# Three PSUM banks of two kinds of piece used as one ring

## The chip, the cores and the metric

The kernel runs on one core of one Trainium2 chip. The metric is the device time of one execution in microseconds (us); where several executions were timed, their median is given. The core's engines are PE (matrix products, with PEld loading the stationary operand), DVE (elementwise work and reductions), ACT (activations and copies), POOL (elementwise work on SBUF and indirect DMA) and SP (which issues most DMAs). PE writes its products to PSUM[...]; DVE and ACT empty them.

## What is computed

Two layers of a transformer-like block in float32, on 2048 tokens of 512 channels. The reference, cut to its skeleton:

```python
xn = layernorm(x)
x = x + lightning_attention(xn, qkv_w, out_w, gate_w, norm_w) + moe(xn, router, experts, shared)
xn = layernorm(x)
x = x + attention(xn, Wqkv, bqkv, Wo, bo) + routed_low_rank(xn, A, B, Wr)
```

In layer 0, the attention has 32 heads of 128 with exponential decay and no softmax:

```python
qkv = silu(h @ qkv_w.T)
scores = einsum('bhnd,bhmd->bhnm', q, k) * decay
attn = einsum('bhnm,bhmd->bhnd', scores, v)      # in blocks, with a carried state
out = (sigmoid(h @ gate_w.T) * norm_w * rms_normalized(attn)) @ out_w.T
```

The mixture has 16 experts of inner width 128, of which each token takes two, and a shared one: `h = silu(x @ w1 + b1) * (x @ w2 + b2)`, then `gate * (h @ w3 + b3)`. Layer 1 has softmax attention with one head of 128 and 64 low-rank adapters of rank 16, of which each token takes sixteen.

## The kernel before

The tokens are cut into four chunks of 512 (`NCH`). The kernel runs in three stages.

The opening normalizes and transposes the chunks, computes the shared expert and the router's choice, and works out at which row of a buffer each token goes for its experts.

Layer 0 then goes over the chunks i, and in each over eight groups g of four heads (a "unit"), and in each over seven parts p (`ORDER`), because the big projections to q, k, gate and v are made with Strassen's seven products of half-size blocks instead of eight (the `Outer` class; `product`, line 667, is its matrix product; sums of blocks are made on DVE and POOL). Chunk 0 uses the plain products and makes the weight sums that later chunks reload. Between the parts, the kernel places smaller pieces of work from a list: `later(after, f)` puts a piece down for so many slots later, and `slot()`, called after every block product, takes one piece that is due. So the order on PE is written out by hand. The pieces are:

- `Quarter.scores` (lines 770 and 771): q times k for two heads, read by DVE, which multiplies by the decay (line 97 is the helper `tt` through which all elementwise operations of two tensors go, on DVE or POOL)
- `Quarter.attend` (lines 782 and 783): scores times v, read by ACT (squares for the norm, lines 794 and 797) and by DVE (gate, line 802)
- `Unit.project` (line 859) and, in chunk 0 and the last unit, `project_plain` (line 879): the output projection, added to the accumulator `acc` by DVE, or copied by ACT in the first group (lines 867 and 888)
- `Expert.turn`, `up` and `down` (lines 707, 717 and 729) for one tile of 128 expert rows: a transpose (read by DVE, line 709), the two up products (read by ACT for `h`, line 724, and then by DVE for `he`, line 725), and the down product, copied by ACT (line 734).

Layer 1 goes over the chunks again. For each it runs low-rank products by the same seven-product scheme (`seven`, lines 1423 and 1493), and between them the pieces of attention: the transposes (line 243), the router (1305), q and k (1299), v (1345), scores and softmax (1357), the gates' transpose (1379), the probabilities' transpose (1442), and the output product `attended` (1468). The router, q, k, scores and so on of the next chunk are called its "head".

A piece gets its PSUM bank from a pool by a tag. A tag has a number of buffers, and a piece that asks for one waits until the piece that had it is released, that is, until its last reader is done. The eight banks before: two for tag `a`, one each for `b` and `e` (the big products), two for `sc`, one for `o` (scores times v) and one for `y`. Tag `sc` serves scores, the experts' transposes and up products, half of the output projections and all the head pieces of layer 1; tag `y` serves the experts' down products, the other half of the output projections, and line 1468. In `project`, for example:

```python
py = ps_sc() if p in ("p7", "p5", "p2") else ps_y()
```

A scheduler orders the instructions from the program's order, and may move one ahead of another that still has to wait for a buffer. In layer 0 the engines' orders follow the list of pieces.

Of the kernel before, what the change touches and what calls it, by code (L numbers as in the profile page):

```python
# [9 lines left out]
FP = mybir.dt.float32  # L10
# [8 lines left out]
P = 128  # L19
# [47 lines left out]
def block_kernel(  # L67
# [38 lines left out]
    ps = ctx.enter_context(tc.tile_pool(name="ps", bufs=1, space=PSUM))  # L106
# [21 lines left out]
        return stage.tile([P, C + WROW], FP, tag="xw", name=name)  # L128

    def ps_sc():  # L130
        return ps.tile([P, 512], FP, tag="sc", name="ps_sc", bufs=2)

    def ps_o():
        return ps.tile([P, 512], FP, tag="o", name="ps_o", bufs=1)

    def ps_y():
        return ps.tile([P, 512], FP, tag="y", name="ps_y", bufs=1)


    opening = ExitStack()  # L140
# [124 lines left out]
    def route(xT, ge, sel):  # L265

        full = [P, TPC, E]
        pl = ps_sc()
        for t in range(TPC):
            for c in range(NC):  # L270
# [58 lines left out]
    def shared_down(i, hT):  # L329
        xc = xs[i]  # L330
        pg = ps_sc()
        for t in range(TPC):
            nc.tensor.transpose(pg[0 : E + 1, bass.ts(t, P)], gates[i][:, t, :], ident)
        gT = work.tile([E + 1, CH], FP, tag="geT", name="geT", bufs=1)
        nc.scalar.copy(gT, pg[0 : E + 1, :])
        for t in range(TPC):
            py = ps_mm()
            mm(py, gT[:, bass.ts(t, P)], b3_t, start=True, stop=False)
            for e in range(SH):
                mm(py, hT[:, e, bass.ts(t, P)], w3sh[:, e, :], start=False, stop=(e == SH - 1))  # L340
            tt(xc[:, t, :], py, xc[:, t, :], ALU.add)
# [135 lines left out]
    for i in range(NTT):  # L477
        tt(cum[:, i + 1, :], cum[:, i, :], sel_all[:, i, :], ALU.add)
    pp = ps_sc()
    flat = "p t e -> p (t e)"  # L480
    at = NTT * E
# [118 lines left out]
    with tc.tile_pool(name="attn", bufs=1) as attn:  # L600
# [89 lines left out]
        class Expert:  # L690
# [36 lines left out]
            def down(self):  # L727
                py = ps_y()
                mm(  # L729
                    py, self.he, self.we[:, 2 * NC * INTER : 2 * NC * INTER + C],  # L730
                    start=True, stop=True,
                )
                ye = attn.tile([P, C], FP, tag="sum", name="ye", bufs=3)
                nc.scalar.copy(ye, py)
                nc.sync.dma_start(out=yd[bass.ts(self.j, P), :], in_=ye)
# [75 lines left out]
        class Unit:  # L811
# [43 lines left out]
            def project(self, p):  # L855
                py = ps_sc() if p in ("p7", "p5", "p2") else ps_y()
                for t in range(2):
                    for hh in range(2):
                        mm(  # L859
                            py[:, bass.ts(t, S)], self.O[p][:, hh, bass.ts(t, P)], self.wo[p][:, hh, :],  # L860
                            start=(t == 0 and hh == 0), stop=(hh == 1), skip_group_check=True,
                        )
                if self.i not in acc:
                    acc[self.i] = accp.tile([P, 7, 2, C // 2], FP, tag="acc", name="acc")
                o = acc[self.i][:, SEVEN.index(p)].rearrange("p t c -> p (t c)")
                if self.g == 0:
                    nc.scalar.copy(o, py)
                else:
                    add(o, py, o)
                if p == "p3":  # L870
                    if (self.i, self.g) == (NCH - 1, NG - 2):
                        combine(self.i)
                    self.done()

            def project_plain(self, b, pair, gT, t):
                py = ps_sc() if t else ps_y()
                for h in range(2):
                    for hh in range(2):
                        mm(  # L879
                            py[:, bass.ts(h, S)], gT[:, hh, bass.ts(t, P)], self.wo[pair, h][:, hh, :],  # L880
                            start=(h == 0 and hh == 0), stop=(hh == 1), skip_group_check=True,
                        )
                if self.i not in acc:
                    acc[self.i] = accp.tile([P, 7, 2, C // 2], FP, tag="acc", name="acc")
                o = acc[self.i][:, 2 * b : 2 * b + 2, t]
                py = py.rearrange("p (h c) -> p h c", h=2)
                if self.g == 0 and pair == 0:
                    nc.scalar.copy(o, py)
                else:
                    add(o, py, o)  # L890
                if (pair, b, t) == (1, 0, 1):
                    self.done()
# [710 lines left out]
```

## Time and profile before

| | us |
|---|---|
| median of 3 runs | 2904.78 (2901.41 to 2913.6) |
| the profiled execution | 2910.55 |
| its span in the profile | 2908.9 |

By stage, from the busy times by stretch of the profiled execution:

| stretch, us | what | PE busy | DVE busy | ACT busy | POOL busy | PE clock granted |
|---|---|---|---|---|---|---|
| 0 to 177 | opening | 151.0 | 109.8 | 54.0 | 85.1 | 0.92 |
| 177 to 809 | layer 0, chunk 0 | 618.4 | 377.0 | 145.3 | 363.2 | 0.99 |
| 809 to 1400 | layer 0, chunk 1 | 576.1 | 285.2 | 227.5 | 323.2 | 1.00 |
| 1400 to 2000 | layer 0, chunk 2 | 594.6 | 298.1 | 238.3 | 303.5 | 1.00 |
| 2000 to 2601 | layer 0, chunk 3 | 580.0 | 305.9 | 230.5 | 328.6 | 0.99 |
| 2601 to 2909 | layer 1 | 291.0 | 177.3 | 57.5 | 65.9 | 0.99 |

The chunks' borders are rounded. A wait row of the profile reads "engine, tile and line that waited <- engine, tile and line that ended it: us in total, times, longest". A row of the timeline has start, length, engine, line, operation, the tiles as out<-in, and in brackets how long the engine was idle before it and what ended that. A float32 product appears as two matrix instructions.

### The profile page before, as it was taken

To read this page: it belongs to the slowest core of one execution; us is meant where nothing else is said; L and a number is where in the kernel's file an instruction comes from. 1 tells how busy PE (TensorE), PEld (TensorE's weight loads), DVE (VectorE), ACT (ScalarE), POOL (GpSimd) and SP (SyncE) were. 2 spreads that over 40 slices of the span, in tenths; PEclk is the share of its full clock that TensorE was granted. 3 is DMA by queue.
4 is the path that set the end of the run, shared out by engine and by line. 5 is a ranking of instruction groups with operands and counts; after the bars stand their busy time and mean duration, and the time that the engine had idled before them with its cause. 6 is when DMAs were issued, how large, how long until landed. Compare 5 with 4: busy or idle time off the path is not lost.

```text
span 2908.9 us, 49460 instructions
## 1 busy us (share of the span) xinstructions
PE 2811.0 (97%) x19864; PEld 2570.9 (88%) x19864; DVE 1553.3 (53%) x2615; ACT 953.1 (33%) x1683; POOL 1469.4 (51%) x1213
## 2 busy tenths in 40 slices
PE   8989999999999999999999999999999989999999
PEld 4469999999989999999999999999999979987877
DVE  7555666666544545444545555555445455558463
ACT  3312222221244333333443333333433334332111
POOL 4535666565445555555645555445444665554110
PEclk9999999999999999999999999999999999999999
DMA  7788998888987777777777777777777776653111
GB/s 263 291 307 329 350 350 344 342 333 329 368 319 258 277 251 262 260 264 277 285 263 258 257 259 260 261 280 282 282 257 257 282 297 225 224 213 96 60 60 60
DMA packets 161942, 763.20 MB, mean 262 GB/s; under 512 B 18209, under 2 KB 24225, under 8 KB 109874
## 3 DMA queue, kind: packets, MB, share of 16 engines
q1 hardware_dynamic: 149826, 706.25, 65.7%
q0 software_dynamic: 11888, 53.79, 5.3%
q8 instruction: 157, 2.57, 0.4%
q14 instruction: 71, 0.58, 0.1%
HBM read 596.14 MB, written 163.05 MB: 261 GB/s over the span
## 4 chain that ended last, share of the span: by engine, by line
PE 78%; DVE 9%; DMA 4%; issue 4%; POOL 2%; ACT 1%; SPq 0%; DVEq 0%; POOLq 0%; ACTq 0%
PE ps_a L667 22%; PE ps_e L667 11%; PE ps_b L667 7%; PE ps_y L859 5%; PE ps_sc L859 4%; PE ps_o L782 3%; PE ps_sc L770 3%; PE ps_sc L717 2%; PE ps_y L879 2%; PE ps_sc L879 2%; DVE c L97 2%; PE ps_a L1493 2%; PE ps_o L783 2%; PE ps_sc L771 2%; PE ps_y L729 1%
## 5 line engine op out<-in xcount | busy, mean ns | idle before, releaser
L667 PE MATMUL ps_a<-xt,w 128*128 128x128 f32 x5376 | 752.9, 276 | 15.0 <-DVE r L97 7.4
L667 PEld LDWEIGHTS ps_a<-xt,w 128*128 128x128 f32 x5376 | 683.1, 193 | 36.4 <-issue 14.9
L97 POOL TENSOR_TENSOR c<-c,r 128x512 f32<-128x512 f32 x240 | 323.7, 1366 | 186.3 <-DVE r L97 138.7
L745 ACT ACTIVATE c<-c 128x512 f32<-128x512 f32 x256 | 161.3, 630 | 656.7 <-DVE c L97 360.2
L667 PE MATMUL ps_e<-xt,w 128*128 128x128 f32 x2688 | 374.3, 275 | 2.0 <-DVE c L97 1.3
L97 POOL TENSOR_TENSOR c<-c 128x512 f32<-128x512 f32 x216 | 270.7, 1269 | 184.6 <-DVE c L97 182.6
L97 POOL TENSOR_TENSOR w<-w 128x512 f32<-128x512 f32 x224 | 292.9, 1322 | 133.4 <-DVE w L97 67.8
L667 PEld LDWEIGHTS ps_e<-xt,w 128*128 128x128 f32 x2688 | 344.7, 192 | 12.4 <-issue 4.1
L97 POOL TENSOR_TENSOR sums<-sums,sq 128x512 f32<-128x512 f32 x120 | 154.3, 1286 | 386.5 <-ACT sq L797 386.1
L667 PE MATMUL ps_a<-w,xt 128*128 128x128 f32 x1792 | 346.9, 275 | 0.0
L997 ACT COPY cp<-ps_a 128x512 f32<-128x512 f32 x336 | 195.0, 580 | 426.9 <-PE ps_a L667 426.9
L667 PEld LDWEIGHTS ps_a<-w,xt 128*128 128x128 f32 x1792 | 272.6, 192 | 0.0
L97 DVE TENSOR_TENSOR c<-ps_a,c 128x512 f32<-128x512 f32 x232 | 158.0, 687 | 214.5 <-PE ps_a L667 213.5
L667 PE MATMUL ps_b<-xt,w 128*128 128x128 f32 x1680 | 236.3, 277 | 4.8 <-ACT c L1011 4.2
L802 DVE SCALAR_TENSOR_TENSOR gT<-ps_o,nw,c 128x256 f32<-128x256 f32 x256 | 111.9, 479 | 226.5 <-ACT sq L797 222.4
L667 PEld LDWEIGHTS ps_b<-xt,w 128*128 128x128 f32 x1680 | 216.9, 194 | 16.1 <-issue 5.5
L859 PE MATMUL ps_y<-wo,gT 128*128 128x256 f32 x736 | 175.4, 381 | 0.6 <-DVE acc L97 0.6
L667 PE MATMUL ps_e<-w,xt 128*128 128x128 f32 x896 | 173.5, 275 | 0.0
L770 PE MATMUL ps_sc<-c 128*128 128x256 f32 x512 | 154.1, 383 | 11.3 <-DVE he L725 7.7
L97 DVE TENSOR_TENSOR s<-ps_sc,decay 128x384 f32<-128x384 f32 x256 | 139.1, 551 | 39.0 <-PE ps_sc L771 37.7
L782 PE MATMUL ps_o<-s,c 128*128 128x256 f32 x512 | 153.8, 382 | 4.3 <-DVE s L97 4.2
L859 PEld LDWEIGHTS ps_y<-wo,gT 128*128 128x128 f32 x736 | 132.8, 190 | 15.5 <-issue 0.7
(307 smaller groups left out, 4768.1 us busy)
## 6 DMA issues: line engine op xcount, KB each, us to landing
w<-in_w_att_dram SPq DMA_DIRECT2D x128, 1024.0 KB
st<-in_w_att_dram SPq DMA_DIRECT2D x32, 1024.0 KB
wo<-in_w_out_dram SPq DMA_DIRECT2D x113, 256.0 KB
decay<-dec SPq DMA_DIRECT2D x64, 384.0 KB
w<-ws0p SPq DMA_DIRECT2D x12, 1792.0 KB
w<-ws1p SPq DMA_DIRECT2D x12, 1792.0 KB
w<-ws2p SPq DMA_DIRECT2D x12, 1792.0 KB
w<-ws3p SPq DMA_DIRECT2D x12, 1792.0 KB
```

Source lines behind the costliest of these rows:

```text
L97: (eng or nc.vector).tensor_tensor(o, a, b, op)
L667: mm(bank[:, bass.ts(ty, P)], a, b, start=(first and ty == 0), stop=True, skip_group_check=True,)
L717: mm(pu[:, bass.ts(n, P)], w12[:, n, c, :], self.xeT[:, c, :], start=(c == 0), stop=(c == NC - 1),)
L745: nc.scalar.activation(qk, qk, AF.Silu)
L770: mm(p[:, 0:S], self.c[:, 2 * hh, P : 2 * P], q, start=True, stop=True)
L771: mm(p[:, S : S + P], self.c[:, 2 * hh + 1, P : 2 * P], q[:, 1, :], start=True, stop=True,)
L782: mm(po[:, bass.ts(hh, S)], v[:, 0, :], self.s[:, hh, 0:S], start=True, stop=False)
L783: mm(po[:, hh * S + P : (hh + 1) * S], v[:, 1, :], self.s[:, hh, S:], start=False, stop=True,)
L802: nc.vector.scalar_tensor_tensor(gT[:, h, :].rearrange("p (t n) -> p t n", t=2), po[:, bass.ts(h, S)].rearrange("p (t n) -> p t n", t=2), ...
L859: mm(py[:, bass.ts(t, S)], self.O[p][:, hh, bass.ts(t, P)], self.wo[p][:, hh, :], start=(t == 0 and hh == 0), stop=(hh == 1), skip_group_c ...
L879: mm(py[:, bass.ts(h, S)], gT[:, hh, bass.ts(t, P)], self.wo[pair, h][:, hh, :], start=(h == 0 and hh == 0), stop=(hh == 1), skip_group_ch ...
L997: nc.scalar.copy(c, bank)
```

## The change

The tag `sc` gets a third buffer, and `ps_y()` hands out a buffer of `sc` instead of one of its own tag, which is gone. The total stays at eight banks. All pieces that took `sc` or `y` now share three banks and take them in turn.

```diff
     def ps_sc():
-        return ps.tile([P, 512], FP, tag="sc", name="ps_sc", bufs=2)
+        return ps.tile([P, 512], FP, tag="sc", name="ps_sc", bufs=3)

     def ps_o():
         return ps.tile([P, 512], FP, tag="o", name="ps_o", bufs=1)

     def ps_y():
-        return ps.tile([P, 512], FP, tag="y", name="ps_y", bufs=1)
+        return ps_sc()
```

Pieces that were named `ps_y` in the profile are named `ps_sc` after the change.

## The prediction

> **What bounds the kernel now.** I read the page first, then the waits of PE, then the stretches around those waits in order of time. The page's first part:
>
> ```profile
> PE 2811.0 (97%) x19864; PEld 2570.9 (88%) x19864; DVE 1553.3 (53%) x2615; ACT 953.1 (33%) x1683; POOL 1469.4 (51%) x1213
> ```
>
> PE has work in 97% of the span, and no other engine is above 53%. So 2908.9 - 2811.0 = 97.9 us of PE's idle time is about all that a new bank order can give back. The waits of PE (us in total, times, longest) say who ended it:
>
> ```profile
> PE ps_sc L859 <- DVE gT L802: 7.8, 1, 7.8
> PE ps_sc L770 <- DVE he L725: 7.7, 7, 3.2
> ...
> PE ps_y L729 <- DVE acc L97: 5.8, 6, 1.0
> ...
> PE ps_y L1468 <- DVE spare L97: 4.0, 2, 2.3
> PE ps_y L729 <- ACT acc L867: 3.8, 3, 1.5
> ...
> PE ps_sc L770 <- DVE acc L97: 3.2, 1, 3.2
> ```
>
> The reader is to see two kinds of wait. L859 waits for gT, which it multiplies: data. L770 does not read he, and L729 and L1468 do not read acc or spare: each waits until the reader named has emptied the bank that it is to write. With the small rows of the same kind (0.6 and 0.3 in layer 0, 0.6 and 0.4 in layer 1) these bank waits make 21.4 us in layer 0 (19 stalls) and 5.0 us in layer 1. From 879 to 1347 us they come as a pair in every unit of 77.8 us. One pair:
>
> ```profile
> 926.59 0.35 DVE L725 SCALAR_TENSOR_TENSOR he<-ps_sc,xw,h 128x128 f32<-128x128 f32 x1 [0.95 <-ACT h L724]
> 927.09 0.67 PE L770 MATMUL ps_sc<-c 128*128 128x256 f32 x2 [0.74 <-DVE he L725]
> ...
> 956.70 0.35 DVE L725 SCALAR_TENSOR_TENSOR he<-ps_sc,xw,h 128x128 f32<-128x128 f32 x1 [4.54 <-ACT h L724]
> 956.97 0.68 DVE L97 TENSOR_TENSOR acc<-ps_y,acc 128x512 f32<-128x512 f32 x1
> 957.70 0.30 PEld L729 LDWEIGHTS ps_y<-xw,he 128*128 128x128 f32 x2 [1.16 <-DVE acc L97]
> 957.70 1.12 PE L729 MATMUL ps_y<-xw,he 128*128 128x512 f32 x2 [0.97 <-DVE acc L97]
> ```
>
> At 927.09 scores wait for the expert's up product, two ps_sc pieces back, which DVE could not read before ACT had made h. At 957.70 the down product waits for the one ps_y bank; but it reads he too, and he was ready only at 957.05, 0.65 us before. The longest bank wait, and what it costs besides:
>
> ```profile
> 578.01 4.71 DVE L97 TENSOR_TENSOR w<-w 128x512 f32<-128x512 f32 x3
> 582.65 0.68 DVE L97 TENSOR_TENSOR acc<-ps_sc,acc 128x512 f32<-128x512 f32 x1
> 583.25 0.67 DVE L97 TENSOR_TENSOR c<-ps_e,c 128x512 f32<-128x512 f32 x1
> 583.38 1.18 PE L770 MATMUL ps_sc<-c 128*128 128x256 f32 x2 [3.24 <-DVE acc L97]
> ```
> ```profile
> 583.30:587.00 3.70, 3.62 (x15) 3.44 (x16) 3.50 (x7) 0.00 (x0) 3.00 (x3) 0.54 0.42 49
> 587.00:600.00 13.00, 13.00 (x102) 12.54 (x101) 8.08 (x12) 0.60 (x1) 8.33 (x7) 1.00 0.98 394
> ```
>
> The last two are the busy times by stretch (PE, PEld, DVE, ACT, POOL, then the granted clock): after the stall PE ran at 0.54, so it lost another 3.70 x 0.46 = 1.7 us.
>
> [...] the trace agrees after the stalls of 3.24 us at 583 and 3.25 at 848 (0.63 from 848.5 to 853.1, 1.7 us lost), and shows half clock after the 2.28 us one at 2647 too[...].
>
> **The change, part by part.** No computing instruction or DMA is added or removed, and no queue but PE's gets new conditions in layer 0: there the order on all five engines is the old one. What changes is which piece each of the 711 pieces of the two kinds waits for. Before: the ps_sc piece two back, or the ps_y piece one back. After: in 696 cases the piece three back, whichever kind (in layer 1 a dozen take the bank that came free first).
>
> What is taken away, layer 0. A stall's gap understates it: running products overlap (six start in 0.83 - 0.28 = 0.55 us, so 0.11 apart, each lasting 0.275), so each costs its gap plus 0.16. The 19 stalls cost 21.4 + 19 x 0.16 = 24.5 us. Does the new condition stall instead? I set the first product of each piece against the end of the last reader of the piece three back, both from the trace of before. The middle distance is 8 us, the smallest in layer 0 is 0.98 us, and for the stalled pieces it is 4.3 us or more. So no new bank wait in the places as they are. What stays is data: the seven L729 stalls between 879 and 1347 keep their wait for he, 1.13 lost and only 0.60 gained each, so 7 x 0.53 = 3.7 us stay. That leaves 20.8 us, and with the two half-clock windows (2 x 1.7) 24.2 us.
>
> What is late next. PE gains only until it meets another bank whose reader does not follow PE.
> - At 583: DVE is held by its weight sums until 582.65 whatever PE does. PE would be 5.1 us early (3.4 + 1.7) at its next ps_e group (587.57 before, so 582.5), and that bank is read by DVE until 583.92. It waits about 1.5 us there. Net 3.6.
> - At 848: the ps_a group of 852.40 needs the bank that ACT copies until 849.06, in a chain that started before the stall: 3.3 of 5.1 us stay.
> - The six L770 stalls of 0.9: the next tight bank (933.8) has 0.75 us to spare, so up to 0.16 is lost each, 0.9 in all.
> - L729 at 1455 and 2046 (1.6 each): ACT is behind there, and the ps_a group at 1460.65 has 0.65 us to spare: 1.9 of 3.2 is lost.
> Sum given back: 1.5 + 1.8 + 0.9 + 1.9 = 6.1. Layer 0 gains 24.2 - 6.1 = 18.1 us. Later the other engines follow, since they are idle about half the time and wait for PE's products.
>
> Layer 1 (from 2601). Here the order moves, because a piece may be placed while a third bank is free. Five low-rank products (0.43 us each) that stood before and between the first head's products now follow them; PE has 2.48 us to wait there for k, which ACT makes after its softmax work for the router, and two of the five filled PE's time before that wait: 0.9 us lost. The three L1468 stalls of the first chunk (2.8 us of gaps and a half-clock window) go, but DVE has no idle time there between 2643 and 2652, and the next ps_e group needs its copy of 2651.04: I count 0.5. At 2797 the stall goes (1.68) and with it 1.14 us for which DVE itself waited for that product. The group behind it, though, waits for DVE already:
>
> ```profile
> 2803.27 0.68 DVE L97 TENSOR_TENSOR cp<-ps_e,cp 128x512 f32<-128x512 f32 x1
> ...
> 2804.01 1.13 PE L1423 MATMUL ps_e<-t,fa 128*128 128x256 f32 x4 [1.66 <-DVE cp L97]
> ```
>
> so I count 1.1 there, and 0.6 for the L243 wait at 2812. Sum -0.9 + 0.5 + 1.1 + 0.6 = 1.3, with 5 either way, since the order of DVE and ACT moves too. The two built programs also differ in PE's waits on its own earlier products (380 for 326); all stand four or more products back, and the waits of PE charge those of before with 0.8 us in all, so I take nothing, with 2 us as the upper bound.
>
> Total 18.1 + 1.3 = 19.4 us. The profiled execution took 2910.55 us (span 2908.9), 5.8 above the median of the runs, 2904.78. Taken from the median: 2904.8 - 19.4 = 2885.4, say 2886.
>
> **Rivals.** A: everything is given back elsewhere. For: DVE and ACT chains do end several of the stalls, and the give-back above was followed only to the next tight bank. Against: DVE 53% and ACT 33% busy, and no tight bank between the pairs. If two thirds of layer 0's 24.2 us are given back and layer 1 gives nothing, 8 us stay: 2897. B: little is given back, and layer 1's waits go as well: 24.2 + 5.0 + 1.7 = 31 us, 2874. Against it: the DVE work at 578 and 2643 does not depend on PE. C, slower: layer 1's order. Its three head chains have less low-rank work between them, and DVE, which bounds the chunk boundaries (32.6 us busy of 36 between 2780 and 2816), now makes gathered-row sums ahead of the copy that PE waits for. Price: the five products of 0.43, three boundaries of about 1.5, and two half-clock windows of 1.7, together 10 us; it decides only if layer 0 keeps under 10 of its 18. With 4 kept: 2911. That the change does not do what it says can be left aside: the ring of three is in the built program.
>
> **How the numbers follow.** Forecast 0.52, A 0.30, B 0.12, C 0.06. A measurement of this kernel tells 0.5%, 14.5 us, from no change. The forecast's own spread (14 to 25 us) is nearly all on the faster side, A mostly within the bound, B faster, C half within it and half beyond: faster 0.60, same 0.36, slower 0.04. The range goes from B's end, 2872, to just short of no gain, 2903: the runs of before differ by 12 us among themselves.
>
> **What would show it.** PE's idle time falls from 97.9 to about 80 us; rows of L770, L729 and L1468 waiting for he, acc or spare vanish, but for about 0.4 us each of L729 waiting for he. The clock stays at 1.00 around 583 and 848. Stalls of 1 to 2 us appear at a ps_e group near 583 and a ps_a group near 848, ended by DVE and ACT. Units of 77.8 us become about 76.4. I am wrong if those units keep their length, or if layer 1, 308 us now, grows by more than 5.

## The result and the profile after

| | before | changed |
|---|---|---|
| median, 10 runs each, us | 2909.24 (2896.75 to 2920.75) | 2890.01 (2882.67 to 2903.62) |
| the profiled execution, us | 2910.55 | 2889.33 |
| its span, us | 2908.9 | 2887.6 |

The ratio is 0.9944, with a 95% interval of 0.992 to 0.9967. Measured again beside later runs, the changed kernel gave 0.9953 (0.994 to 0.9966). In the profile after, PE does the same work in less time; the page's first part:

```profile
PE 2808.7 (97%) x19864; PEld 2571.3 (89%) x19864; DVE 1555.9 (54%) x2615; ACT 952.4 (33%) x1683; POOL 1467.2 (51%) x1213
```

PE's idle time is 2887.6 - 2808.7 = 78.9 us, 19.0 less than before. The waits of PE (us in total, times, longest):

```profile
PE ps_e L1423 <- DVE cp L97: 8.8, 2, 6.5
PE ps_sc L859 <- DVE gT L802: 5.2, 1, 5.2
...
PE ps_sc L729 <- DVE he L725: 4.1, 8, 1.6
...
PE ps_e L667 <- DVE c L97: 3.3, 4, 1.2
```

There is no row of L770 or L1468 any more, and L729 waits only for he, which it multiplies. (In a second profiled execution of the changed kernel one wait of L1468 for spare, of 1.1 us, is left.) One unit of chunk 1 in the timeline, the one that was shown of before around 927:

```profile
875.09 1.13 PE L729 MATMUL ps_sc<-xw,he 128*128 128x512 f32 x2 [0.31 <-DVE he L725]
...
921.38 0.60 PE L770 MATMUL ps_sc<-c 128*128 128x256 f32 x2
921.41 0.35 ACT L724 ACTIVATE h<-ps_sc,xw 128x128 f32<-128x128 f32 x1
921.79 0.35 DVE L725 SCALAR_TENSOR_TENSOR he<-ps_sc,xw,h 128x128 f32<-128x128 f32 x1 [0.95 <-ACT h L724]
...
951.30 1.12 PE L729 MATMUL ps_sc<-xw,he 128*128 128x512 f32 x2 [0.36 <-DVE he L725]
```

DVE still waits 0.95 us for ACT's h before it can make he, as before. But scores (L770) now start before he is made, because they write to another bank. The unit takes 76.2 us (875.1 to 951.3 at L729) instead of 77.8. At the two long stalls of before:

```profile
581.59 0.60 PE L770 MATMUL ps_sc<-c 128*128 128x256 f32 x2
...
587.82 0.94 PE L667 MATMUL ps_e<-xt,w 128*128 128x128 f32 x6 [1.19 <-DVE c L97]
...
847.56 1.12 PE L729 MATMUL ps_sc<-xw,he 128*128 128x512 f32 x2 [1.60 <-DVE he L725]
```
```profile
581.00:586.00 5.00, 5.00 (x43) 4.90 (x42) 5.00 (x5) 0.00 (x0) 4.45 (x3) 1.00 0.92 358
847.00:852.00 5.00, 4.44 (x32) 3.91 (x33) 3.26 (x6) 4.01 (x8) 4.40 (x5) 1.00 0.92 333
```

The granted clock (third number from the end of the lower lines) is 1.00 in both places, where it had been 0.54 and 0.63 after the stall; and in each a shorter stall has come in its place, of 1.19 and 1.60 us.

Where the time went is read best by taking the same instruction of PE in both traces (layer 0's order is the same) and subtracting its starts. The table gives how much each kernel gained on before's profiled execution in each stretch, in us; the last two columns are the first two experiments below.

| stretch of before, us | changed | ring in layer 0 only | ring in layer 1 only |
|---|---|---|---|
| 0 to 177, opening | -4.3 | -5.4 | -1.2 |
| 177 to 570 | 0.2 | 0.0 | 0.7 |
| 570 to 720 (stall at 583) | 2.7 | 3.1 | 0.6 |
| 720 to 809 | 2.3 | 3.4 | 3.6 |
| 809 to 870 (stall at 848) | 3.3 | 3.3 | -1.3 |
| 870 to 1350 (a pair of stalls a unit) | 10.1 | 10.1 | -0.1 |
| 1350 to 2370 | 3.9 | 2.9 | 0.0 |
| 2370 to 2578 | 5.3 | 5.2 | 1.4 |
| 2578 to the end, layer 1 | -2.3 | 2.6 | -0.1 |
| sum | 21.2 | 25.2 | 3.6 |

### The profile page after: what moved, and what is told of

The parts are those of the page before. It is cut to its first block, busy times and chain, and to the rows that moved or that the text cites. A ratio compares the mean times of both kernels' runs of the same rounds, so it can differ in the third digit from the quotient of the medians.

```text
span 2887.6 us, 49441 instructions
## 1 busy us (share of the span) xinstructions
PE 2808.7 (97%) x19864; PEld 2571.3 (89%) x19864; DVE 1555.9 (54%) x2615; ACT 952.4 (33%) x1683; POOL 1467.2 (51%) x1213
## 4 chain that ended last, share of the span: by engine, by line
PE 84%; DVE 7%; DMA 4%; issue 2%; POOL 2%; ACT 1%; SPq 0%; DVEq 0%; POOLq 0%; ACTq 0%
PE ps_a L667 24%; PE ps_e L667 12%; PE ps_sc L859 9%; PE ps_b L667 7%; PE ps_sc L879 4%; PE ps_o L782 4%; PE ps_sc L770 3%; PE ps_sc L717 3%; PE ps_a L1493 2%; PE ps_o L783 2%; PE ps_sc L771 2%; PE ps_sc L729 1%; DVE c L97 1%; PE ps_a L1423 1%; DVE r L97 1%
## 5 line engine op out<-in xcount | busy, mean ns | idle before, releaser
L667 PE MATMUL ps_a<-xt,w 128*128 128x128 f32 x5376 | 751.0, 276 | 18.0 <-DVE r L97 9.3
L667 PEld LDWEIGHTS ps_a<-xt,w 128*128 128x128 f32 x5376 | 681.5, 192 | 38.3 <-issue 14.0
L667 PE MATMUL ps_e<-xt,w 128*128 128x128 f32 x2688 | 374.0, 275 | 3.5 <-DVE c L97 3.3
L97 POOL TENSOR_TENSOR w<-w 128x512 f32<-128x512 f32 x224 | 293.5, 1325 | 137.9 <-DVE w L97 74.3
L667 PEld LDWEIGHTS ps_e<-xt,w 128*128 128x128 f32 x2688 | 344.2, 192 | 14.1 <-DVE c L97 4.2
L667 PE MATMUL ps_a<-w,xt 128*128 128x128 f32 x1792 | 346.5, 275 | 0.0
L859 PE MATMUL ps_sc<-wo,gT 128*128 128x256 f32 x1288 | 306.6, 381 | 5.2 <-DVE gT L802 5.2
L667 PEld LDWEIGHTS ps_a<-w,xt 128*128 128x128 f32 x1792 | 272.2, 192 | 0.0
L97 DVE TENSOR_TENSOR acc<-ps_sc,acc 128x512 f32<-128x512 f32 x208 | 143.1, 689 | 232.7 <-PE ps_sc L859 163.5
L859 PEld LDWEIGHTS ps_sc<-wo,gT 128*128 128x128 f32 x1288 | 233.5, 191 | 30.7 <-DVE gT L802 5.4
L667 PE MATMUL ps_b<-xt,w 128*128 128x128 f32 x1680 | 235.8, 277 | 4.7 <-ACT c L1011 4.2
L667 PEld LDWEIGHTS ps_b<-xt,w 128*128 128x128 f32 x1680 | 216.5, 193 | 15.8 <-issue 5.5
L667 PE MATMUL ps_e<-w,xt 128*128 128x128 f32 x896 | 173.2, 275 | 0.0
```

Source lines behind the costliest of these rows:

```text
L97: (eng or nc.vector).tensor_tensor(o, a, b, op)
L667: mm(bank[:, bass.ts(ty, P)], a, b, start=(first and ty == 0), stop=True, skip_group_check=True,)
L859: mm(py[:, bass.ts(t, S)], self.O[p][:, hh, bass.ts(t, P)], self.wo[p][:, hh, :], start=(t == 0 and hh == 0), stop=(hh == 1), skip_group_c ...
```

## The experiments

Theory T: the gain is the removal of bank waits in layer 0, at their own price. The rivals are named with the runs. Kernels that carry the helper of the first experiment have their lines moved by 15 or 16, so that L785 is L770, L744 is L729, L874 is L859, L682 is L667, L1439 is L1423 and L1484 is L1468.

**The ring in one layer alone.** Both kernels have before's tags and take them in turn where `ring_on` says so; it is switched just before layer 1's first head. (`bank_sc()` hands out before's two buffers of `sc`, `bank_y()` its one of `y`.)

```diff
+    def in_turn(own):
+        if not ring_on[0]:
+            return own()
+        turn_of_ring[0] += 1
+        return (bank_y, bank_sc, bank_sc)[turn_of_ring[0] % 3]()
...
     def ps_sc():
-        return ps.tile([P, 512], FP, tag="sc", name="ps_sc", bufs=2)
+        return in_turn(bank_sc)
...
     def ps_y():
-        return ps.tile([P, 512], FP, tag="y", name="ps_y", bufs=1)
+        return in_turn(bank_y)
...
+    ring_on[0] = False
     head = Head(0)
```

> The ring of three is used in layer 0 only; layer 1 has the old banks (two for the one kind, one for the other). Theory T (the gain is the bank waits of layer 0): the whole gain of the change stays, 18 to 24 us, a ratio of 0.992 to 0.994 to the kernel before, and PE's waits at lines 770 and 729 for he or acc are gone, while the waits of line 1468 for spare (4 to 5 us) stay. Since layer 1 lost 1.7 us with the ring, this version should be as fast as the changed kernel or up to 2 us faster. Rival R (the gain comes from layer 1's other order): 1.000.

Measured: 2883.07 us median, a ratio of 0.9919 (0.9895 to 0.9942). As expected, PE has no wait of L770 for he or acc and none of L729 for acc left, and L1468 still waits for spare (4.2 us). The other way round, with `ring_on` false first and true in layer 1:

> The ring of three is used in layer 1 only; layer 0 has the old banks. Theory T: a ratio of 0.999 to 1.001, layer 1 between 0 and 3 us longer: its line 1468 no longer waits for spare, but DVE is behind there and line 1423 waits for cp instead (about 9 us in two waits). The 21 us of bank waits in layer 0 stay. Rival R (the gain comes from layer 1's other order): 0.994.

Measured: 2908.02 us median, 1.0013 (1.0002 to 1.0024), that is 0.6 to 7 us slower than before. The waits of PE with the ring in layer 1 only:

```profile
PE ps_sc L785 <- DVE he L740: 7.7, 7, 3.2
PE ps_e L1439 <- DVE cp L97: 6.7, 2, 4.4
PE ps_sc L874 <- DVE gT L817: 6.6, 1, 6.6
PE ps_y L744 <- DVE acc L97: 5.8, 6, 1.0
```

Layer 0's bank waits are what they were before, and layer 1's longer wait for cp is there (2.8 us in two before). So the whole gain lies in layer 0, rival R falls, and the ring in layer 1 costs a little. The third column of the table is of use for a second reason: this kernel has before's banks in layer 0, so what it gained there, 4.9 us between 177 and 2578, is not the ring. Most of it (3.6) stands at 726, where before's profiled execution waited 2.04 us for gT and then ran at a clock of 0.66 for 5 us, and this one did not wait; in the nine other profiled executions that wait is anything from 0 to 1.65 us. Against this kernel the changed one gained 27.8 - 4.9 = 22.9 us in layer 0. Five profiled executions in all have the ring of three in layer 0 with PE's order unchanged. From 177 to 2578 they gained 25.5 to 28.8 us on before's execution, so 20.6 to 23.9 on this one.

**The up products in the single bank.** Before's tags, and in `Expert.up`:

```diff
-                pu = ps_sc()
+                pu = ps_y()
```

> The banks of before, two for the one kind and one for the other, but the experts' up products take the single bank (y) in place of one of the pair (sc). The order of the instructions is that of before. Theory T (it is a matter of which reader stands before a piece in its bank, three pieces back being enough): the waits of line 770 for he go (from 12 to about 4 us in all), but line 859's output products and line 729 then stand behind an up product in the one bank, and by the times of the trace line 859 gets some 40 us of waits of a kind that it had not; slower than before by 10 to 30 us, 1.004 to 1.010. Rival S (taking the up products off the pair of banks is what gains): 0.996 or lower.

Measured: 2938.04 us median, 1.012 (1.0093 to 1.0146). The waits of PE:

```profile
PE ps_y L859 <- DVE he L725: 35.6, 17, 3.0
...
PE ps_sc L770 <- DVE acc L97: 1.9, 2, 1.2
```

L770 no longer waits for he, but the output products do, 17 times. Between 870 and 2578 this kernel fell from 10.5 us ahead of before to 25.2 behind, 35.7 us, close to what that row says. What was expected came out, a little past its dear end (33 us slower for 10 to 30); rival S falls.

**A ring of two.** The changed kernel with `bufs=2` for `bufs=3`, one of the eight banks being left unused.

> All pieces of both kinds in one ring as in the changed kernel, but of two banks[...]. Theory T (the third bank back is what counts): by the times of the changed kernel's trace every piece two back leaves 23 us of bank waits in layer 0, as much as before (22), so a ratio of 0.998 to 1.002. Rival U (sharing itself, that a piece is not tied to a kind, is the gain): 0.994 to 0.996. Rival V (a bank less costs more than the order of turns gains): above 1.005.

Measured: 2895.14 us median, 0.996 (0.9949 to 0.9971): about half of the changed kernel's gain, at the edge of what rival U gave and outside T's. The waits of PE say why:

```profile
PE ps_sc L770 <- DVE he L725: 7.7, 7, 3.2
...
PE ps_sc L859 <- DVE s L97: 5.4, 1, 5.4
...
PE ps_sc L729 <- DVE he L725: 2.6, 7, 0.4
```

The waits of L770 for he are all there: scores stand two pieces behind the up product, and two banks are too few. The waits of L729 for acc are gone: they came from the tie of the down product to the one bank y, and the turn of two removes them; in the trace that is 0.6 us in each of seven units. So U is right for one of the two waits of the pair; the other stays when two banks are taken in turn. The step of T that failed is the count of 23 us of waits. The trace has 16.3 us of bank waits in layer 0, and the longest, 5.4 at L859, only replaces waits that stood behind it before: those for s (2.36), c (1.32) and cp (0.86) are gone and the one for gT is 2.0 shorter. PE was 5.3 us behind before's execution ahead of this place and 4.7 behind after it. Why the other 7 us of the count did not appear is open. (This profiled execution took 2912.78 us, 17 above its median, because it lost 16 us before 177: the clock in 120 to 180, third from the end, was 0.72. From 177 to 2578 it gained 12.2 us on before's.)

```profile
120.00:180.00 60.00, 56.85 (x109) 21.24 (x110) 18.41 (x38) 7.57 (x10) 17.27 (x31) 0.72 0.61 232
```

**Two and one, but sorted otherwise.** Before's tags; the up products take y, and all output projections take sc. Layer 1 is as before.

```diff
-                pu = ps_sc()
+                pu = ps_y()
...
-                py = ps_sc() if p in ("p7", "p5", "p2") else ps_y()
+                py = ps_sc()
...
-                py = ps_sc() if t else ps_y()
+                py = ps_sc()
```

> No ring: two banks of the one kind and one of the other, as before, but with other pieces in them. The experts' up and down products have the single bank to themselves in layer 0, and all output projections, scores and transposes share the pair. Theory T (only the distance in time between a bank's reader and its next writer counts): the changed kernel's trace, taken over to these banks, leaves 10.9 us of bank waits in layer 0 of the 21.6, of which 6 are at output products (lines 859 and 879) that wait for data next anyway, as in the ring of two; so the waits at 729 for acc go, those at 770 fall to about 4 us, and the time is 12 to 20 us under before, 0.993 to 0.996. Rival W (the ring's freedom to take any bank is needed): 0.999 or more.

Measured: 2885.69 us median, 0.9941 (0.9919 to 0.9963), the changed kernel's own ratio, without a ring. The waits of PE:

```profile
PE ps_sc L859 <- DVE s L97: 4.3, 1, 4.3
...
PE ps_y L729 <- DVE he L725: 4.1, 8, 1.6
PE ps_sc L770 <- DVE acc L97: 3.9, 3, 2.5
```

Rival W falls: what counts is how long ago a bank's last reader was due when the next piece comes, and a sorting that puts the slowly read pieces (up, down) behind one another does that nearly as well. In layer 0 (177 to 2578) it gained 21.3 us on before's execution, the ring of three 25.5 to 28.8; layer 1, where it has before's banks, gained 5.1 us in this execution and lost 2.3 in the changed kernel's, which would make up for that. The pairs and the stall at 848 gave as much as with the ring (13.3 us from 809 to 1350 for 13.2 to 13.4); from 2370 to 2578, where L859 now waits for s, it gained 1.6 us and the ring 3.9 to 5.7.

**The data wait that stays.** The ring in layer 0 only, and the down product one slot later.

```diff
-            later(14, e.down)
+            later(15, e.down)
```

> The ring of three in layer 0 only, and the experts' down product due one slot later (15 for 14). Theory T: what stays of the stalls at line 729 is its wait for he (4.1 us in 8 stalls in the changed kernel), a wait for data that a later place removes; so this row goes and the time is 3 to 5 us under that of the ring in layer 0 with 14: a ratio of 0.9900 to 0.9915. If the bank behind it (the one that down leaves later) now comes late, the row goes and the time stays at 0.992.

Measured: 2885.76 us median, 0.9928 (0.99 to 0.9957): not better than with 14 by the median, though the interval does not exclude what was expected. The row L729 waiting for he is gone, and these have grown in its place (1.6 and 1.1 us with 14):

```profile
PE ps_e L682 <- DVE c L97: 5.2, 4, 1.8
PE ps_a L682 <- ACT cp L1012: 5.0, 5, 2.4
```

A miss for T, and what its second case said: behind the wait for he stand the banks of the big products, which DVE and ACT empty. From 870 to 1350 this kernel gained 12.6 us on before's execution (10.1 with 14), which is what the row promised, but from 1350 to 2370 it lost 1.0 where the ring with 14 had gained 2.9.

**What layer 1 loses.** Between the first score product of layer 1 and the end, the changed kernel took 290.8 us, the ring in layer 0 only 286.4. The changed kernel measured again:

> The changed kernel once more, beside the next two on the same chip, so that layer 1's part can be read from pairs. Theory T: 0.993 to 0.9955, and 2 to 5 us slower than a kernel with the ring in layer 0 alone, because DVE reaches the copy for line 1423 later when the three banks are shared in layer 1. If layer 1's difference in the profiled executions (290.8 us from the first score product to the end with the ring, 286.4 without) was a matter of chance, no difference.

Measured: 2890.46 us median, 0.9953 (0.994 to 0.9966), 4.7 us slower than the ring in layer 0 only with the later down product, and with the same wait for cp (8.3 us in two, the longest 6.0). From the first score product on it took 293.5 us. With the ring in layer 1 only that part took 289.7, and in the five kernels with before's banks and gate buffers in layer 1 it took 286.2 to 291.3. The ring's mean is 3 us longer; but the five have the same code there and differ by 5, so one execution alone shows little. DVE around the long wait, in the changed kernel:

```profile
2621.03 0.69 DVE L97 TENSOR_TENSOR hg<-cp,spread_g 128x512 f32<-128x512 f32 x1 [2.50 <-DMA spread_g<-gd]
...
2622.44 3.81 DVE L236 TENSOR_SCALAR spare<-x,mv,rstd 128x512 f32<-128x512 f32 x4
...
2630.84 0.68 DVE L97 TENSOR_TENSOR cp<-ps_e,cp 128x512 f32<-128x512 f32 x1
...
2631.57 3.78 PE L1423 MATMUL ps_e<-t,fa 128*128 128x256 f32 x8 [6.49 <-DVE cp L97]
```

DVE waits 2.50 us for gate rows, then normalizes the next chunk and multiplies the gathered rows, and only then comes to the copy that PE waits for. The stall costs more than its gap: the granted clock was 0.51 from 2629 to 2636. In the five kernels with the old banks in layer 1 DVE did not wait there. To see whether that wait makes the stall, the gate rows got a third buffer, and `GT` gave up its own to make room:

```diff
-            GT = work.tile([K, CH], FP, tag="GT", name="GT", bufs=1)
+            GT = work.tile([K, CH], FP, tag="S", name="GT")
...
-            sp = work.tile([P, 2, CH], FP, tag="spread", name="spread_g")
+            sp = work.tile([P, 2, CH], FP, tag="spread", name="spread_g", bufs=3)
```

> The changed kernel with a third buffer for the gate rows of layer 1 (spread_g), whose room is made by letting the small gate tile (GT) share the buffers of the probabilities. PE's order is that of the changed kernel; on DVE the product that reads ps_a and frees the first gate rows again stands ahead of the one that waits for the second. Theory L (layer 1 lost because DVE, before it normalizes, waits 2.5 to 3.1 us for gate rows whose load could start only when a buffer came free): that wait goes in the first chunk, the stall of line 1423 for cp falls from 6 to 6.5 us to 3 to 4, layer 1 becomes 2 to 3 us shorter than in the changed kernel, a ratio of 0.9935 to 0.9945. Rival (the ring's order on PE alone makes the 6 us, DVE being full of its own work there): the stall stays at 5 to 6.5, ratio as the changed kernel's 0.995. Sharing the buffers of the probabilities may add a wait of ACT of about 1 us.

Measured: 2889.62 us median, 0.9945 (0.9923 to 0.9967). The same place:

```profile
2619.71 0.69 DVE L97 TENSOR_TENSOR hg<-cp,spread_g 128x512 f32<-128x512 f32 x1 [0.72 <-DMA spread_g<-gd]
...
2621.13 3.82 DVE L236 TENSOR_SCALAR spare<-x,mv,rstd 128x512 f32<-128x512 f32 x4
...
2629.53 0.68 DVE L97 TENSOR_TENSOR cp<-ps_e,cp 128x512 f32<-128x512 f32 x1
...
2630.26 3.78 PE L1423 MATMUL ps_e<-t,fa 128*128 128x256 f32 x8 [5.48 <-DVE cp L97]
```

DVE's wait is 1.8 us shorter, the stall only 1.0, and layer 1 as a whole was no shorter (294.1 us). The ratio alone would fit theory L as well as its rival; by the stall, which stayed in the rival's 5 to 6.5 us, theory L falls. DVE is full from 2620.3 to 2630.2 with work of its own, 8.1 us of it the normalizing and the gathered rows. That PE stands before the copy because of the ring's order is what is left, but no run changed that order alone. The ring of two is a hint: in its execution the copy comes behind fewer of the gathered rows, the waits for cp are 2.3 us in three, and the part from the first score product on took 284.8 us. Both edits together, the ring in layer 0 only and the third gate buffer:

> The ring of three in layer 0 alone, together with the third buffer for the gate rows in layer 1. If the ring in layer 0 gives 22 us and the gate rows' waits in layer 1 (14.5 us of DVE's idle time in 9 waits) stand on the path for some 2 us: 0.991 to 0.992, the best of all. If DVE's waits there are covered by PE's other work: as the ring in layer 0 alone, 0.992.

Measured: 2887.32 us median, 0.9942 (0.9922 to 0.9963), no better than without the gate buffer. In its trace DVE waits 1.47 us for gate rows just before the normalizing, and PE's L1468 waits 9.1 us in four for spare, the longest 5.5, where the ring in layer 0 alone had 4.2. So neither case named beforehand came out: the buffer moved a wait. The lowest ratio of all is that of the ring in layer 0 alone, 0.9919; its interval overlaps the changed kernel's two, so that it is better, by some 7 us, is likely and not certain.

## Why the prediction was right

The mechanism was the one named: bank waits in layer 0. The time came 4 us above the forecast because before's median was 4.5 us higher in the ten runs than in the three that the forecast started from. The gain itself, 19.2 us between the medians for 19.4, agrees better than its parts do: below, layer 0 gave 4.8 us more than was counted and layer 1 3.6 less, and the interval of the gain reaches from 9.6 to 23.3 us. That these errors cancel so nearly is luck. By the prediction's steps, with the gain against the kernel that has before's banks in layer 0 (second experiment), so that chance differences between single executions drop out as far as they can:

| step | predicted | measured |
|---|---|---|
| the stall at 583, net | 3.6 | 2.1 to 720, 0.8 to 809 |
| the stall at 848, net | 3.3 | 4.6 (3.3 against before) |
| the pairs, 870 to 1350 | 6 x 0.9 + 7 x 0.6 - 0.9 = 8.7 | 10.2 |
| 1455 and 2046, net | 1.3 | 3.9 (all of 1350 to 2370) |
| small waits at 2407 and 2573 | 0.6 + 0.3 + 2 x 0.16 = 1.2 | 3.9 (all of 2370 to 2578) |
| layer 0 | 18.1 | 22.9 (with -0.5 before 570) |
| layer 1 | +1.3, 5 either way | -2.3 against before |

- The stall and what it costs besides: right. The pairs were worth 0.91 and 0.60 us, the prediction had 0.9 and 0.60; of the 0.9 that the six stalls of L770 were to give back, nothing was. At 583 PE was 5.15 us earlier by 587, for 5.1. The clock stayed at 1.00 at 583 and 848.
- Given back at the next tight bank: right at 583 (1.19 us at the ps_e group for the 1.5 named) and in size at 1455, though one group later and behind DVE instead of ACT (the ps_a group waits 1.78 us for r, 0.39 before); at 2046 nothing was given back. It was not followed far enough at 583: waits of 0.83 for gT, 0.49 for c and 0.33 for s came behind it. At 848 the size was right against before (the clock granted from 840 to 870 was 0.89 in the second experiment for before's 0.94, which makes its 4.6) and the place was not: the 1.60 us stand at the down product, which waits for he. The prediction looked for the next tight bank there and not for the next tight datum.
- The seven waits for he that stay: predicted 0.37 us each plus a restart, seen at 0.31 to 0.37.
- How far single executions can be trusted: in the five with the ring of three in layer 0, the stall at 848 (809 to 870) gave 3.2 to 3.3 us against before and the pairs (870 to 1350) 10.0 to 10.1 every time, but the stretch from 570 to 720 anything from 0.4 to 5.2.
- Near 2390 the step was mis-sized: L859's wait for gT was counted as data and left alone. Against the second experiment it shrank from 6.6 to 5.2 us, and the bank wait of 1.4 behind it (0.6 in before's execution) went. Why gT came earlier relative to PE was not tried.
- Layer 1 was the weakest step. Its stalls at L1468 went, as said, but the copy behind them took over more than they had cost: 8.8 us in two waits for cp (2.8 before), where the prediction allowed for DVE having no idle time between 2643 and 2652 and still counted 0.5 and 1.1 of gain. (One of the L1468 stalls that it counted there, 0.42 us at 2642, stands in the profile as "issue", so nothing shows it to be a wait for a bank.) Measured by itself, the ring in layer 1 costs 0.6 to 7 us. That sign lay inside the 5 us left for it.
- The opening, in which PE's order is the same and its waits hardly change, differs by 4.3 us between the two profiled executions. It hides as much of the gain in the spans as layer 1 does.

Of the rivals, A (two thirds given back) falls with layer 0's 22.9 us, and with the lowest of the five executions too (20.6). B was right about layer 0 and wrong about layer 1. C has its mechanism, the ring in layer 1 with DVE as the bound, at 0.6 to 7 us for its 10, and without the small gain in layer 0 that it needed.

Taking three banks in turn paid in layer 0 (20.6 to 23.9 us against the second experiment) and not in layer 1. The ring of two was faster than before (0.996) with seven banks for before's eight, and two and one, sorted otherwise, were nearly as fast in layer 0 as the ring of three (21.3 us for 25.5 to 28.8), while the same eight banks with the up products in y were 1.2% slower than before. The number of banks in use does not tell the time alone; which piece follows which counts as much.

## What to carry to other kernels

Before giving a piece another bank, put each piece's first write against the end of the last reader that would stand in its bank then, from the trace: that told the pairs to within 0.2 us each, and the loss from putting the up products in y (40 us of waits for 35.6 measured), though it overcounted the ring of two (23 for 16). Then follow the engine that is released to its next wait, for data as well as for banks. Where another engine is full, as DVE is at layer 1's chunk boundaries, taking a bank wait away moved PE's stall to that engine's next product (8.8 us of waits for cp where there had been 2.8); there the change is likely better left out.

## What was not expected of the hardware

Single executions differ in the opening by more than what is looked for. At 177 us of before's time the changed kernel's own two profiled executions stood 4.3 and 7.9 us behind before's, and those of the other kernels, whose openings differ little, between 3.4 ahead and 16.1 behind; the clock granted from 120 to 180 was 0.72 in the slowest, 0.95 in before and 0.97 in the first execution of the changed kernel, whose clock from 60 to 120 was 0.83 for before's 0.89. A stage's gain is therefore safer read from instruction to instruction within the stage than from two spans.

The half clock does not hang on the length of a wait alone. In before's execution the waits of PE of 3.24 us at 583, 2.04 at 726, 3.25 at 848 and 2.28 at 2647 were each followed by 3.41 us at a granted clock of 0.50 (from 583.46, 726.82, 849.70 and 2648.52), and the wait of 2.48 us at 2619 was not: there the clock was 1.00 from 2619 to 2624. So the wait of 2.04 us had as much half clock behind it as that of 3.24 us, and a longer one than it had none. In the changed kernel the clock was 0.50 from 2581.35 to 2588.18, though PE had been busy without a break for the 3.41 us ahead. What sets the half clock off is not shown by these runs.
